# One graph-attention layer on one core: k made transposed by one product a block, and turned back

## The chip, the cores and the metric

The kernel runs on one core of one Trainium2 chip. The metric is the device time of one execution in microseconds (us). A core has five engines that run their own instruction streams in order and wait for each other by semaphores: TensorE (PE, matrix products and transposes, its weight loads listed apart as PEld), VectorE (DVE), ScalarE (ACT), GpSimd (POOL), and SyncE (SP), which issues DMAs here. PE works from SBUF and writes into PSUM; DVE and ACT read both.

## The reference

There are 12,500 nodes with 128 features, 212,500 edges sorted by `dst`, and 128 features for each edge. Eight heads of 16 features each:

```python
h = relu(layernorm(x))
q = h @ Wq.T + bq
k = edge_attr @ Wk.T + bk
v = h @ Wv.T + bv
in_m, out_m, diag_m = sum(q[src] * k), sum(q[dst] * k), sum(q[src] * q[dst])   # over each head
score = (softmax_by_dst(in_m / 4) + softmax_by_dst(out_m / 4) + softmax_by_dst(diag_m / 4)) * edge_weight ** lam
out = x + leaky_relu(segment_sum(score * v[dst], dst) @ Wo.T + bo, 0.1)
```

## The kernel before

After a first part over the nodes (their norm, `q`, and the two tables `q_table` and `q3_table` in DRAM), the main loop runs over 415 blocks of 512 edges. A block is four columns (`JN = 4`) of 128 edges, one edge a partition. Five blocks (`S = 5`, one of each fifth of the edge list) make one step `t`, and `g = 5 t + s` counts blocks. The features of five blocks come in one DMA into `ea` (`fetch_edges`, 1,280 KB).

For each block the loop needs three things in the layout "edge on the partition": `qs = q[src]`, `qd = q[dst]` and `k`.

- `gather` (line 652) fetches `q[src]`: four indirect DMAs a block on POOL (line 656), `LOOK = 12` blocks ahead. Each of the four also waits for a product of PE recorded in `behind`, so that the gathers run close behind PE's products: the gathers that are issued in iteration `g` wait for four places in PE's order of iteration `g - 1`.
- `spread_q` (line 1137) makes `q[dst]`: four bf16 products of one-hot rows (`oh`, made by ACT in `one_hots`, lines 1118 and 1119) with a window of the table, and ACT copies the result to SBUF (line 1144).
- `turn` (line 1121) transposes the edge features: four f32 transposes into the PSUM tile `eT_ps` (line 1124, one buffer), which ACT copies into `eT` (line 1126). `project` (line 1129) makes `k`: one bf16 product of ones with the bias (line 1131), then four f32 products with `eT` as the weights and `wk` as the moving operand (line 1133), all into `k_ps` (two buffers). A f32 product is two MATMULs in the trace, a transpose is one.

`logits` (line 1147) is DVE's: three products of 128x512 elements (lines 1152 to 1154, the first needs `qd` and `k_ps`, the last frees `k_ps`) and one reduction (line 1155).

The order of each engine is fixed by hand: `pin` ties every instruction behind the one that was recorded before it on the same engine. In iteration `g`, PE gets `spread_q(g + 1)`, `project(g + 1)`, `turn(g + 2)`, and then the work that comes once a step: transposes of the logits (`s = 0`), of the maxima (`s = 2`), `show_ends` (`s = 3`), `to_rows` with 16 f32 MATMULs (`s = 4`), and the nodes' products. ACT gets, in the same order, the copy of `qd_ps`, the copy of `eT_ps`, the two passes of `one_hots(g + 3)` and the work of the step. PE's order therefore asks of ACT once a block: the transposes of one block are copied by ACT before the product of that block, one iteration later, can run.

Of the kernel before, what the change touches and what calls it, by code (L numbers as in the profile page):

```python
# [472 lines left out]
def ordered_path(ctx: ExitStack, tc: tile.TileContext, flag, x, src, dst, edge_attr, edge_weight,  # L473
# [87 lines left out]
    wq, wv, wk, wo = [consts.tile([P, F], F32, name=n) for n in ("wq", "wv", "wk", "wo")]  # L561
    b3 = consts.tile([3, 3, F], BF, name="b3")
    bv3, bk3, bo3 = [b3[:, i, None, :].to_broadcast([3, JN, F]) for i in range(3)]
    bq_all = consts.tile([P, F], F32, name="bq_all")

    inv = consts.tile([P, NI], F32, name="inv")
# [23 lines left out]
    def pin(inst):  # L590

        engine = str(inst.ins.engine)
        if engine in pinned:
            tc.add_manual_dep(inst.ins, pinned[engine], mybir.DependencyInfo(
                mybir.DependencyClass.NoSync, mybir.DependencyReason.DATA), reason="in order")
        pinned[engine] = inst.ins.name
        return inst
# [47 lines left out]
    def fetch_edges(t):  # L645
        if t < G:
            ea = eas[t] = load.tile([P, S, JN * F], F32, name="ea")
            pin(nc.sync.dma_start(
                ea, edge_attr[:end * BE, :].rearrange("(s b p j) f -> p s b (j f)", s=S, b=G, p=P)
                [:, :, t, :]))  # L650
# [46 lines left out]
    with tc.tile_pool(name="prep", bufs=1) as prep, \  # L697
# [24 lines left out]
        rows_in(dst_r[:, 1:RC + 1], dst, nc.sync)  # L722
        pin(nc.gpsimd.dma_start(dst_r[1:, 0:1], dst[RC - 1:(RW - 1) * RC:RC, None]))
        pin(nc.gpsimd.dma_start(dst_r[:RW - 1, RC + 1:], dst[RC:(RW - 1) * RC + 1:RC, None]))
        b_row = prep.tile([1, 3, F], F32, name="b_row")
        for i, b in enumerate((bv, bk, bo)):
            pin(nc.sync.dma_start(b_row[:, i, :], b[None, :]))
# [286 lines left out]
    class Nodes:  # L1014
# [39 lines left out]
        def turn(self, to):  # L1054
            for b in range(self.n):
                pin(nc.tensor.transpose(to[:, b, :], self.h[:, b, :], ident))
            if self.hT is None:
                self.hT = fin.tile([P, JN, P], F32, name="hT")
            pin(nc.scalar.copy(self.hT[:, :self.n], to[:, :self.n]))
# [48 lines left out]
    with tc.tile_pool(name="work", bufs=2) as work, \  # L1108
            tc.tile_pool(name="scan", bufs=2) as scan, \
            tc.tile_pool(name="ps", bufs=1, space=PSUM) as ps:  # L1110
        ks, eTs, qds, q_ps, ohs, lTs = {}, {}, {}, {}, {}, {}

        def one_hots(g):

            if g < end:
                oh = ohs[g] = work.tile([K3, BE], BF, name="oh", bufs=5)
                d = st[g // S]["relb"][:, g % S, :]
                pin(nc.scalar.activation(d, d, AF.Abs, bias=before[:K3]))  # L1118
                pin(nc.scalar.activation(oh, d, AF.Relu, bias=1.0, scale=-1.0))  # L1119

        def turn(g):
            eT_ps = ps.tile([P, JN, P], F32, name="eT_ps", bufs=1)
            for j in range(JN):
                pin(nc.tensor.transpose(eT_ps[:, j, :], eas[g // S][:, g % S, j * F:(j + 1) * F], ident))  # L1124
            eT = work.tile([P, JN, P], F32, name="eT", bufs=3)
            pin(nc.scalar.copy(eT, eT_ps))  # L1126
            eTs[g] = eT

        def project(g):
            k_ps = ks[g] = ps.tile([P, JN, F], F32, name="k_ps", bufs=2)  # L1130
            pin(nc.tensor.matmul(k_ps, ones3, bk3, start=True, stop=False))  # L1131
            for j in range(JN):
                pin(nc.tensor.matmul(k_ps[:, j, :], eTs[g][:, j, :], wk, start=False,  # L1133
                                     stop=(j == JN - 1)))
            del eTs[g]

        def spread_q(g):
            s, d = g % S, st[g // S]
            qd_ps = q_ps[g] = ps.tile([P, JN, F], F32, name="qd_ps", bufs=2)
            for j in range(JN):  # L1140
                pin(nc.tensor.matmul(qd_ps[:, j, :], ohs[g][:, j * P:(j + 1) * P],  # L1141
                                     d["win"][:, s, :], start=(j == 0), stop=(j == JN - 1)))
            qds[g] = work.tile([P, JN, F], F32, name="qd")
            pin(nc.scalar.copy(qds[g], qd_ps))  # L1144
            del ohs[g]
# [226 lines left out]
                        pin(nc.gpsimd.memset(of.more, 0.0))  # L1372

        def hold(of, name):
            of.held = ps.tile([P, JN, F], F32, name=name, bufs=1 if name == "eT_ps" else 2)
            of.product(of.held, bv3, wv)

        products = str(mybir.EngineType.PE)
# [3 lines left out]
        fetch_rows(1)  # L1382
        one_hots(0)
        turn(0)
        spread_q(0)
        project(0)
        turn(1)
        one_hots(1)
        one_hots(2)
        for g in range(end):  # L1390
            s, t = g % S, g // S
            nodes_before(t, s)
            gather(g + LOOK)
            if s == 0:
                fetch_edges(t + 1)
            if g + 1 < end:
                spread_q(g + 1)
                behind[g + 1, 0] = pinned[products]
                project(g + 1)
                behind[g + 1, 1] = pinned[products]  # L1400
            if g + 2 < end:
                turn(g + 2)
                behind[g + 1, 2] = pinned[products]
            logits(g)
            one_hots(g + 3)
            if s == 0:
                if t > 0:
                    turn_logits(t - 1)
                    scan_on(t - 1)
                later(select, t - 2)  # L1410
                later(spread_far, t - 2)
            elif s == 1:
                later(scan_back, t - 2)
                if t == 1:
                    logits_few()
            elif s == 2:
                later(turn_max, t - 2)
                later(powers, t - 2)
            elif s == 3:
                later(show_ends, t - 2)  # L1420
                later(weigh_powers, t - 2)
                fetch(t + 2)
            else:
                later(to_rows, t - 2)
            ahead, k = (t + 2, s - 3) if s > 2 else (t + 1, s + 2)
            if ahead > 1:
                fetch_rows(ahead, [k])
                fetch_places(ahead, [k])
            later(put_rows, t - 2 if s == 4 else t - 3, [(s + 1) % S])
            if t == G - 1:  # L1430
                if 0 < s < 4:
                    select(G - 3 + s)
                elif s == 4:
                    for i in (G - 2, G - 1, G):
                        show_ends(i)
            behind[g + 1, 3] = pinned[products]
            nodes_between(t, s)
            begin_rest(g - (end - LOOK))
            if g < S:
                of = [u for u in range(NU) if g in parts_of(u)]  # L1440
                pin(nc.scalar.dma_start(
                    sums[g][of[0] * UN:(of[0] + len(of)) * UN].rearrange(
                        "(n p) i c -> p n (i c)", p=P),
                    blank[:, None, :].to_broadcast([P, 2 * len(of), 2 * 2 * H3])))
# [6 lines left out]
        last_pair.scores()  # L1451
        last_pair.turn(small([P, JN, P], "node_ps"))
        scan_on(G - 1)
        hold(rest[0], "eT_ps")
        last_pair.project_v(ps.tile([P, JN, F], F32, name="k_ps", bufs=2))
        scan_back(G - 2)
        turn_max(G - 2)
# [84 lines left out]
```

## Time and profile before

| | |
|---|---|
| time, median of 3 runs | 2700.01 us (2693.41 to 2700.97) |
| profiled execution: its own time | 2699.03 us |
| profiled execution: span | 2697.2 us |
| main loop's blocks | 415 |
| POOL, gathers (line 656) | 1660 indirect DMAs, 1580.9 us busy |
| DVE, four instructions of `logits` | 280.7 + 282.7 + 282.9 + 727.5 us busy |

The span is the time from the first to the last instruction of the profiled execution; what lies around it is 1.8 us. "Idle before" in a row names the time in which the engine stood still before the instructions of that group, and what ended it: "remote" is an update of a semaphore that the profile can't put down to an instruction that had just ended, and "issue" a start for which it sees no wait.

### The profile page before, as it was taken

The page shows a single profiled execution, that of the slowest core. Times are in us where ns is not written, and L with a number is a line of the kernel's source. Part 1 is how long each engine was busy: PE and PEld are TensorE (multiplying, and loading weights), DVE is VectorE, ACT ScalarE, POOL GpSimd, SP SyncE. Part 2 cuts the span into 40 slices and gives each one's busy share as a digit, 9 for nine tenths or more (in the row PEclk, how much of TensorE's full clock was granted, in tenths as well). Part 3 has the DMA queues.
Part 4 walks back from the last instruction along what each step waited for, and adds up shares of the span by engine and source line. Part 5 has one row for each costly group of instructions (what it writes and reads, how often), then busy time and mean ns, then how long its engine had stood idle before and what let it go on. Part 6 is the DMA issues. An engine that isn't in the chain of part 4 may idle for free.

```text
span 2697.2 us, 35162 instructions
## 1 busy us (share of the span) xinstructions
PE 1792.3 (66%) x10209; PEld 1446.1 (54%) x10209; DVE 2000.0 (74%) x2582; ACT 1382.5 (51%) x2526; POOL 1616.2 (60%) x1690
## 2 busy tenths in 40 slices
PE   6136666666566676766767667676766767666776
PEld 5125555555455565555555556554555556555564
DVE  7647776777677777776877778778777787777794
ACT  6534554454445554555455455455554555555572
POOL 4656666666666666666666666666666666666610
PEclk9667776777777767787777777777777786877776
DMA  7764445444544454445444444444444444444431
GB/s 214 228 196 125 116 114 140 115 116 122 139 117 124 127 135 121 128 120 145 119 124 124 137 130 123 124 138 126 121 120 142 127 125 123 139 126 125 118 105 52
DMA packets 319110, 351.23 MB, mean 130 GB/s; under 512 B 137530, under 2 KB 238661, under 8 KB 318600
## 3 DMA queue, kind: packets, MB, share of 16 engines
q1 hardware_dynamic: 250141, 233.59, 29.2%
q0 software_dynamic: 53344, 109.11, 16.8%
q10 hardware_dynamic: 15424, 6.19, 0.9%
q8 instruction: 83, 1.36, 0.2%
q14 instruction: 118, 0.97, 0.1%
HBM read 316.50 MB, written 32.17 MB: 129 GB/s over the span
## 4 chain that ended last, share of the span: by engine, by line
PE 43%; issue 16%; ACT 14%; another core or an unknown queue 12%; DVE 11%; DMA 3%; SPq 1%; ACTq 0%; POOL 0%; DVEq 0%; POOLq 0%
PE k_ps L1133 15%; PE w_ps L1286 7%; PE eT_ps L1124 6%; PE qd_ps L1141 5%; PE k_ps L1131 3%; ACT eT L1126 3%; DVE u L1208 2%; ACT qd L1144 2%; ACT relb L1118 2%; PE node_ps L1064 2%; DMA q_table<-q 2%; PE m_ps L1238 2%; ACT oh L1119 2%; DVE prod L1153 1%
## 5 line engine op out<-in xcount | busy, mean ns | idle before, releaser
L656 POOL DMA_INDIRECT qq<-q_table,src_i x1660 | 1580.9, 952 | 916.0 <-issue 371.6
L1133 PE MATMUL k_ps<-wk,eT 128*128 128x128 f32 x3320 | 668.4, 363 | 583.0 <-issue 358.4
L1133 PEld LDWEIGHTS k_ps<-wk,eT 128*128 128x128 f32 x3320 | 567.4, 258 | 740.1 <-issue 457.8
L1155 DVE TENSOR_REDUCE lT<-prod 128x96 f32<-128x1536 f32 x415 | 727.5, 1753 | 14.4
L1126 ACT COPY eT<-eT_ps 128x512 f32<-128x512 f32 x415 | 244.0, 588 | 838.7 <-remote 602.5
L1152 DVE TENSOR_TENSOR prod<-qd,k_ps 128x512 f32<-128x512 f32 x415 | 280.7, 676 | 148.6 <-remote 82.9
L1124 PE MATMUL eT_ps<-ident,ea 128*128 128x128 f32 x1660 | 346.6, 348 | 1.2 <-DVE found L962 1.0
L1141 PE MATMUL qd_ps<-win,oh 126*128 126x128 bf16 x1660 | 191.7, 247 | 208.6 <-DMA q_table<-q 70.6
L1144 ACT COPY qd<-qd_ps 128x512 f32<-128x512 f32 x415 | 240.1, 579 | 152.5 <-remote 42.5
L1118 ACT ACTIVATE relb<-relb,before 126x512 bf16<-126x512 bf16 x415 | 301.8, 727 | 0.0
L1141 PEld LDWEIGHTS <-oh 126*128 126x128 bf16 x1660 | 149.3, 113 | 261.6 <-issue 180.0
L1154 DVE TENSOR_TENSOR prod<-qq,k_ps 128x512 f32<-128x512 f32 x415 | 282.9, 682 | 0.0
L1153 DVE TENSOR_TENSOR prod<-qq,qd_ps 128x512 f32<-128x512 f32 x415 | 282.7, 681 | 0.0
L1208 DVE TENSOR_TENSOR_SCAN u<-far,u,l_ps 120x512 f32<-120x512 bf16 x82 | 105.0, 1280 | 238.4 <-PE k_ps L1133 58.8
L1124 PEld LDWEIGHTS eT_ps<-ident,ea 128*128 128x128 f32 x1660 | 279.1, 186 | 1.7 <-DVE found L962 1.3
L1119 ACT ACTIVATE oh<-relb 126x512 bf16<-126x512 bf16 x415 | 261.5, 630 | 33.8 <-issue 20.6
L1286 PE MATMUL w_ps<-back,sel 128*126 128x144 f32 (+1 forms) x1344 | 229.6, 334 | 26.1 <-ACT sel L1276 13.5
L1286 PEld LDWEIGHTS w_ps<-back,sel 128*126 128x126 f32 (+1 forms) x1344 | 213.9, 230 | 48.2 <-ACT sel L1276 30.7
L1131 PE MATMUL k_ps<-b,ones 3*128 3x512 bf16 x415 | 183.4, 442 | 17.2 <-issue 8.5
L1246 DVE TENSOR_TENSOR back<-lT,m_ps 128x480 f32<-128x480 f32 x83 | 54.1, 652 | 166.3 <-PE eT_ps L1124 73.1
L1226 DVE TENSOR_TENSOR_SCAN m<-far_ps,head,u 120x512 f32<-120x512 f32 x81 | 103.3, 1275 | 0.0
L1291 ACT COPY rows<-w_ps 126x288 f32<-126x288 f32 x84 | 33.0, 393 | 127.7 <-PE qd_ps L1141 62.9
(194 smaller groups left out, 1449.1 us busy)
## 6 DMA issues: line engine op xcount, KB each, us to landing
ea<-in_edge_attr_dram SPq DMA_DIRECT2D x83, 1280.0 KB
relb<-rel_d SPq DMA_DIRECT2D x415, 126.0 KB
qq<-q_table,src_i POOLq DMA_INDIRECT x1660
win<-q_table SPq DMA_DIRECT2D x415, 31.5 KB
far<-far_d SPq DMA_DIRECT2D x84, 120.2 KB
q_table<-q SPq DMA_DIRECT2D x24, 384.0 KB
sums<-rows SPq DMA_DIRECT2D x412, 7.9 KB
q_table<-xq SPq DMA_DIRECT2D x24, 256.0 KB
```

The costliest lines, as they stand in the source:

```text
L656: rows = pin(nc.gpsimd.indirect_dma_start(out=qq[:, j, :], out_offset=None, in_=q_table, in_offset=bass.IndirectOffsetOnAxis(ap=src_i[:, g ...
L1118: pin(nc.scalar.activation(d, d, AF.Abs, bias=before[:K3]))
L1119: pin(nc.scalar.activation(oh, d, AF.Relu, bias=1.0, scale=-1.0))
L1124: pin(nc.tensor.transpose(eT_ps[:, j, :], eas[g // S][:, g % S, j * F:(j + 1) * F], ident))
L1126: pin(nc.scalar.copy(eT, eT_ps))
L1133: pin(nc.tensor.matmul(k_ps[:, j, :], eTs[g][:, j, :], wk, start=False, stop=(j == JN - 1)))
L1141: pin(nc.tensor.matmul(qd_ps[:, j, :], ohs[g][:, j * P:(j + 1) * P], d["win"][:, s, :], start=(j == 0), stop=(j == JN - 1)))
L1144: pin(nc.scalar.copy(qds[g], qd_ps))
L1153: pin(nc.vector.tensor_mul(prod[:, :, 1, :], qqs[g], q_ps[g]))
L1154: pin(nc.vector.tensor_mul(prod[:, :, 0, :], qqs[g], ks[g]))
L1155: pin(nc.vector.tensor_reduce(lTs[t][:, :, s, :], prod.rearrange("p j i (h d) -> p j (i h) d", d=DIM), AX.X, ALU.add))
L1286: pin(nc.tensor.matmul(w_ps[:, i].rearrange("p s c -> p (s c)"), d["sel"][:n, j, lo:lo + 3, :].rearrange("p s w -> p (s w)"), d["back"][:n ...
```

## The change

`k` is now made with the features on the partitions. `project` takes `wk` as the weights and all 512 columns of `eT` as the moving operand, in one f32 product into the PSUM tile `kT_ps`. ACT adds the bias in its copy to `kT` (the bias is one number a partition now, `bk_col`, loaded once at the start). The new `turn_k` transposes `kT` back, four f32 transposes into `k_ps`. The product with ones that brought the bias is gone. `eT_ps` and `kT_ps` share one PSUM buffer (`tag="turned"`, one buffer); `eT` has two buffers in place of three.

The order in iteration `g` becomes `project(g + 2)`, `spread_q(g + 1)`, `turn_k(g + 1)`, `turn(g + 3)`, so `k` runs through one more stage and the features are turned three blocks ahead. The four places that gathers wait for are now the ends of `project`, of `turn_k`, of `turn`, and of the iteration. `fetch_edges` is called at the end of a step for the step after the next.

```diff
+    bk_col = consts.tile([P, 1], F32, name="bk_col")
...
+        pin(nc.sync.dma_start(bk_col, bk[:, None]))
...
         def turn(g):
-            eT_ps = ps.tile([P, JN, P], F32, name="eT_ps", bufs=1)
+            eT_ps = ps.tile([P, JN, P], F32, name="eT_ps", tag="turned", bufs=1)
             for j in range(JN):
                 pin(nc.tensor.transpose(eT_ps[:, j, :], eas[g // S][:, g % S, j * F:(j + 1) * F], ident))
-            eT = work.tile([P, JN, P], F32, name="eT", bufs=3)
+            eT = work.tile([P, JN, P], F32, name="eT")
             pin(nc.scalar.copy(eT, eT_ps))
             eTs[g] = eT
 
         def project(g):
+            kT_ps = ps.tile([P, JN, P], F32, name="kT_ps", tag="turned", bufs=1)
+            pin(nc.tensor.matmul(kT_ps.rearrange("f j p -> f (j p)"), wk,
+                                 eTs.pop(g).rearrange("f j p -> f (j p)"), start=True, stop=True))
+            kTs[g] = work.tile([P, JN, P], F32, name="kT")
+            pin(nc.scalar.activation(kTs[g], kT_ps, AF.Identity, bias=bk_col))
+
+        def turn_k(g):
             k_ps = ks[g] = ps.tile([P, JN, F], F32, name="k_ps", bufs=2)
-            pin(nc.tensor.matmul(k_ps, ones3, bk3, start=True, stop=False))
             for j in range(JN):
-                pin(nc.tensor.matmul(k_ps[:, j, :], eTs[g][:, j, :], wk, start=False,
-                                     stop=(j == JN - 1)))
-            del eTs[g]
+                pin(nc.tensor.transpose(k_ps[:, j, :], kTs[g][:, j, :], ident))
+            del kTs[g]
...
         turn(0)
-        spread_q(0)
         project(0)
         turn(1)
+        spread_q(0)
+        turn_k(0)
+        project(1)
+        turn(2)
...
             gather(g + LOOK)
-            if s == 0:
-                fetch_edges(t + 1)
+            if g == 0:
+                fetch_edges(1)
+            if s == S - 1:
+                fetch_edges(t + 2)
+            if g + 2 < end:
+                project(g + 2)
+                behind[g + 1, 0] = pinned[products]
             if g + 1 < end:
                 spread_q(g + 1)
-                behind[g + 1, 0] = pinned[products]
-                project(g + 1)
+                turn_k(g + 1)
                 behind[g + 1, 1] = pinned[products]
-            if g + 2 < end:
-                turn(g + 2)
+            if g + 3 < end:
+                turn(g + 3)
                 behind[g + 1, 2] = pinned[products]
```

More of the change, by code (lines that the diff above doesn't have):

```diff
@@ L1110, in ordered_path @@
             tc.tile_pool(name="ps", bufs=1, space=PSUM) as ps:
-        ks, eTs, qds, q_ps, ohs, lTs = {}, {}, {}, {}, {}, {}
+        ks, eTs, kTs, qds, q_ps, ohs, lTs = {}, {}, {}, {}, {}, {}, {}
         def one_hots(g):
@@ L1374, in hold @@
         def hold(of, name):
-            of.held = ps.tile([P, JN, F], F32, name=name, bufs=1 if name == "eT_ps" else 2)
+            of.held = ps.tile([P, JN, F], F32, name=name, tag=name, bufs=1 if name == "turned" else 2)
             of.product(of.held, bv3, wv)
@@ L1453, in ordered_path @@
         scan_on(G - 1)
-        hold(rest[0], "eT_ps")
+        hold(rest[0], "turned")
         last_pair.project_v(ps.tile([P, JN, F], F32, name="k_ps", bufs=2))
```

## The prediction

> **What bounds the kernel now.** I read the page's busy shares first, then its groups with their idle times, the list of waits, and last the timelines of PE, ACT and POOL in one stretch of the main loop.
>
> ```profile
> span 2697.2 us, 35162 instructions
> PE 1792.3 (66%) x10209; PEld 1446.1 (54%) x10209; DVE 2000.0 (74%) x2582; ACT 1382.5 (51%) x2526; POOL 1616.2 (60%) x1690
> ...
> L656 POOL DMA_INDIRECT qq<-q_table,src_i x1660 | 1580.9, 952 | 916.0 <-issue 371.6
> L1133 PE MATMUL k_ps<-wk,eT 128*128 128x128 f32 x3320 | 668.4, 363 | 583.0 <-issue 358.4
> ...
> L1126 ACT COPY eT<-eT_ps 128x512 f32<-128x512 f32 x415 | 244.0, 588 | 838.7 <-remote 602.5
> ...
> L1124 PE MATMUL eT_ps<-ident,ea 128*128 128x128 f32 x1660 | 346.6, 348 | 1.2 <-DVE found L962 1.0
> ```
>
> No engine is full, so something makes them wait for each other. Two idle times stand out: 583.0 us of PE before the products of k, and 838.7 us of ACT before the copy of the features that these products need. The list of waits says what ACT waits for, the tile `prod` how long a block takes, and the cores' view the clock:
>
> ```profile
> ACT eT L1126 <- remote: 602.5, 134, 6.9
> ...
> PE qd_ps L1141 <- DMA q_table<-q: 70.6, 1, 70.6
> ```
>
> ```profile
> L1152 DVE TENSOR_TENSOR prod<-qd,k_ps x415: 654/680/690, 160.9 to 2629.1; 128x512 f32<-128x512 f32 x139
> ```
>
> ```profile
> core 0: 2697.2 us, clock 0.750
> ```
>
> A block takes (2629.1 - 160.9) / 414 = 5.96 us. The copy waits only for PE's transposes, and 134 times this wait lasts 602.5 / 134 = 4.5 us. The timelines show why:
>
> ```profile
> 1520.77 0.59 PE L1141 MATMUL qd_ps<-win,oh 126*128 126x128 bf16 x4 [3.04 <-DVE prod L1153]
> 1521.37 0.58 PE L1131 MATMUL k_ps<-b,ones 3*128 3x512 bf16 x1
> 1521.88 2.07 PE L1133 MATMUL k_ps<-wk,eT 128*128 128x128 f32 x8
> 1523.74 1.06 PE L1124 MATMUL eT_ps<-ident,ea 128*128 128x128 f32 x4
> 1524.60 1.01 PE L1238 MATMUL m_ps<-ident,m 120*128 120x120 f32 x4
> ...
> 1541.45 0.39 PE L1141 MATMUL qd_ps<-win,oh 126*128 126x128 bf16 x4
> 1541.77 0.39 PE L1131 MATMUL k_ps<-b,ones 3*128 3x512 bf16 x1
> 1542.08 1.16 PE L1133 MATMUL k_ps<-wk,eT 128*128 128x128 f32 x8
> 1543.08 0.60 PE L1124 MATMUL eT_ps<-ident,ea 128*128 128x128 f32 x4
> 1543.51 0.60 PE L1175 MATMUL l_ps<-ident,lT 128*120 128x128 f32 x4
> ...
> 1545.63 0.60 PE L1124 MATMUL eT_ps<-ident,ea 128*128 128x128 f32 x4
> ...
> 1554.20 2.08 PE L1133 MATMUL k_ps<-wk,eT 128*128 128x128 f32 x8 [6.25 <-issue]
> 1556.07 1.06 PE L1124 MATMUL eT_ps<-ident,ea 128*128 128x128 f32 x4
> ...
> 1559.41 0.60 PE L1124 MATMUL eT_ps<-ident,ea 128*128 128x128 f32 x4
> ```
>
> ```profile
> 1524.84 0.59 ACT L1126 COPY eT<-eT_ps 128x512 f32<-128x512 f32 x1 [2.86 <-issue]
> ...
> 1543.98 0.60 ACT L1126 COPY eT<-eT_ps 128x512 f32<-128x512 f32 x1
> ...
> 1553.57 0.59 ACT L1126 COPY eT<-eT_ps 128x512 f32<-128x512 f32 x1 [6.70 <-remote]
> ...
> 1557.17 0.59 ACT L1126 COPY eT<-eT_ps 128x512 f32<-128x512 f32 x1 [1.26 <-PE eT_ps L1124]
> ...
> 1563.98 0.58 ACT L1126 COPY eT<-eT_ps 128x512 f32<-128x512 f32 x1 [3.21 <-remote]
> ```
>
> ```profile
> 1521.26 0.94 POOL L656 DMA_INDIRECT qq<-q_table,src_i  x1 [2.15 <-issue]
> ...
> 1543.44 0.94 POOL L656 DMA_INDIRECT qq<-q_table,src_i  x1 [1.67 <-PE k_ps L1133]
> ...
> 1550.93 0.94 POOL L656 DMA_INDIRECT qq<-q_table,src_i  x1 [0.30 <-issue]
> 1553.80 0.94 POOL L656 DMA_INDIRECT qq<-q_table,src_i  x1 [1.93 <-remote]
> ...
> 1561.29 0.94 POOL L656 DMA_INDIRECT qq<-q_table,src_i  x1 [0.30 <-issue]
> 1564.15 0.94 POOL L656 DMA_INDIRECT qq<-q_table,src_i  x1 [1.92 <-remote]
> ```
>
> PE's transposes end at 1545.63 + 0.60 = 1546.23, but ACT starts to copy at 1553.57. POOL's last gather of a run ended at 1550.93 + 0.94 = 1551.87, 1.70 us before. The next time: transposes end at 1560.01, POOL's last gather at 1562.23, the copy starts at 1563.98, 1.75 us later. So while POOL issues gathers in a row, the word that PE is done reaches the others late, and it comes through some 1.7 us after POOL has run out of gathers that it may issue (each waits for a place in PE's order). Not at once, though: the transposes that ended at 1524.80 (3.5 us into the run that began at 1521.26), at 1543.68 (0.2 us into the next) and at 1557.13 (3.3 us into the third) were copied 0.04 to 0.30 us later. Those that ended 2.8 us (1546.23) and 6.2 us (1560.01) into a run were not. I call a word from PE that passes "in time", the other "held". This link is read from the rows; what carries it I can't see.
>
> That gives the block's account. Six gathers on from 1543.44 POOL is at 1550.93: 1.248 us each, 4.99 us for a block's four. The other 5.96 - 4.99 = 0.97 us are pauses. A pause in the quoted rows costs (1.67 + 1.93 + 1.92) / 3 - 0.30 = 1.54 us, so 0.97 / 1.54 = 0.63 of the blocks pay one. The loop is set by POOL's runs and the pauses between them, and the pauses by how many hand-overs from PE get through inside one run.
>
> **The change part by part.** *PE's work.* From start to start in the rows, in the fast and the slow stretch: the bias product 0.31 and 0.51 us, the eight MATMULs of k 1.00 and 1.86, four transposes 0.43 and 0.86. The bias goes. The one product streams 512 f32 columns twice. No row has it; from below it is two bf16 passes of 512 columns (2 x 0.31 = 0.62; 2 x 0.51 = 1.02), from above the eight MATMULs as they are. Nearest is a transpose, one f32 pass of 128 columns: 8 x 0.43 / 4 = 0.86 and 8 x 0.86 / 4 = 1.72. I take these. Four transposes are added. Net: -0.31 - 0.14 + 0.43 = -0.02 fast, -0.51 - 0.14 + 0.86 = +0.21 slow; at a mean clock of 0.75 half and half, +0.10 us a block, 40 us over 414. Bounds: -0.26 and -0.49 at the lower price, +0.12 and +0.35 at the upper. PE is busy 66%, so this counts only inside a hand-over.
>
> *ACT's work.* One more pass over 128x512 a block, like line 1126: 588 ns, 415 x 0.588 = 244 us, 51% to 60%. It lies in ACT's idle time (838.7 us before the copy alone). Free of the cover it would cost 244 us. In ACT's order it stands ahead of the copies of `qd` and `eT`, so these now wait for PE's product too.
>
> *The hand-overs.* Before, a block has one in the loop: transposes, word to ACT, copy, product in the next iteration. After, there are two, one behind the other: transposes, word, copy to `eT`, product, word, biased copy to `kT`, and only then the next transposes, since both tiles share one PSUM buffer. From the release of a held word to the end of the next transposes it is now 0.59 (copy) + 1.00 or 1.86 + 0.43 or 0.86 = 2.0 to 3.3 us. After it is 0.59 + 0.86 or 1.72 + 0.32 or 0.60 (`spread_q`, start to start) + 0.43 or 0.86 (`turn_k`) + 0.43 or 0.86 = 2.6 to 4.6 us; the copy to `kT` hides behind `spread_q` and `turn_k` if its own word is in time. So the second word leaves PE some 1.0 us later in POOL's run. The rows have words in time up to 3.5 us and held ones from 2.8 us: a shift of 1.0 us moves it across. DVE gains nothing: `turn_k(g + 1)` stands behind `project(g + 2)` on PE, which waits for the copy.
>
> The price: 0.37 of the blocks pay no pause now. From below none of these is lost, 0 us; from above all, 0.37 x 1.54 = 0.57 us a block, x 414 = 236 us. The quoted cases at 2.8 to 3.5 us split (two pass, one is held), so I take half: 118 us.
>
> The Trainium skill, "Perfetto Trace Analysis", section Matmuls, says that independent groups of products should rotate through PSUM banks, so that emptying one overlaps the next group's products. Here the change does the opposite. By that rule alone every block would pay the copy, 414 x 0.588 = 243 us, near the upper bound; before, the buffer is single too, and the trace shows 1.2 us of waiting ahead of all transposes (line 1124), so a single buffer alone is no wait here.
>
> *What costs nothing.* The load of `bk_col` is one small DMA among the first ones on SP; the two further stages at the start fall into the 70.6 us in which PE waits for the table. `fetch_edges` moves by one iteration, but the transposes that need it move with it, and the buffer that it fills was read three iterations before in both orders. SP holds behind it the windows and rows of later steps, which are as early as before. If that cover fails, a late `ea` would stop PE, at most once in five blocks.
>
> *Sum.* 2699 (the execution: span 2697.2 and 1.8 around it, 1 us under the median) + 118 = 2817, and the median's 1 us: 2818 us.
>
> **The rivals.** *All second words are held* (the shared buffer makes every block pay a pause): 2700 + 236 = 2936. For it: two words a block must pass; against: the first leaves PE early in the run.
>
> *Words pass as now, and only work is added*: PE's 40 us show, 2740. For it: one word passed 3.5 us into a run. Against: the shift of 1.0 us.
>
> *Faster: the wide product is cheap.* If it streams at the bias product's pace, PE does 0.26 (fast) to 0.49 us (slow) less a block ahead of the second word, 0.375 on the mean; 414 x 0.375 = 155 us if all of it is on the path, 78 us at half: 2622. It decides from a product under 0.31 + 1.00 - 0.43 = 0.88 us (fast) and 0.51 + 1.86 - 0.86 = 1.51 us (slow); place: the stretch from the copy to the next transposes. For it: weights are loaded once a block in place of four times, and fewer words from PE could be held. Against: in the rows four f32 transposes take 0.43 us where four bf16 products of the same width (`spread_q`) take 0.32, so f32 columns pass more slowly.
>
> The Trainium skill, "TensorE: Matmul & The Clock Gate", section Back-to-back issue gap, gives 131 ns for 512 columns against 81 ns for 128 in a stream. By it two passes would take an estimated 0.26 us and this rival would hold more than fully. The trace disagrees for f32: here a pass of 128 columns takes 108 to 215 ns (a quarter of the transposes).
>
> *No change*: POOL's own pace and pauses hide all of it, 2700.
>
> **How the numbers follow.** Half of the blocks lose: 0.44, 2818, its own range 2740 to 2900. All lose: 0.12. Work alone: 0.14. Faster: 0.25. No change: 0.05. Within 0.3% (8 us) is no change for a measurement of this kernel. So slower 0.70, same 0.05, faster 0.25. The range of 2630 to 2950 leaves out half of the faster case (0.13) and the far end of the worst (0.06).
>
> **What would show it.** On the page: line 1131 gone, a product of 512 f32 columns with two MATMULs a block, of 0.86 to 1.72 us a pair, PE's share about as before, ACT's near 60%. In the waits: those of the two copies for PE together over 602.5 us, in more than 134 cases. In POOL's timeline: more pauses, runs of four to five gathers rather than of six to seven. I am wrong if the waits that end as "remote" get fewer, if POOL's idle time falls under 916.0 us, or if the extra time appears in DVE's waits for gathered rows.

## The result, and the profile after

| | before | after |
|---|---|---|
| time, median | 2696.71 us (2691.79 to 2700.97, 4 runs) | 2735.79 us (2732.57 to 2739.15, 4 runs) |
| ratio to before on the same chip, 95% interval | | 1.0146 (1.012 to 1.0171) |
| span of the profiled execution | 2697.2 us | 2732.4 us |

Slower by 39 us between the medians, 35 us between the profiled spans. The forecast was 118 us more than before. The page of after, its busy shares and the groups that answer to those of before (busy us, mean ns | idle time before, and what ended most of it):

```profile
span 2732.4 us, 32733 instructions
...
PE 1752.5 (64%) x8964; PEld 1194.8 (44%) x8964; DVE 2005.8 (73%) x2582; ACT 1654.6 (61%) x2941; POOL 1616.0 (59%) x1690
...
L657 POOL DMA_INDIRECT qq<-q_table,src_i x1660 | 1580.8, 952 | 945.6 <-issue 356.3
L1133 PE MATMUL kT_ps<-eT,wk 128*128 128x512 f32 x830 | 594.1, 805 | 514.0 <-ACT eT L1128 298.0
...
L1126 PE MATMUL eT_ps<-ident,ea 128*128 128x128 f32 x1660 | 325.1, 328 | 391.5 <-ACT kT L1136 249.8
L1128 ACT COPY eT<-eT_ps 128x512 f32<-128x512 f32 x415 | 243.2, 586 | 405.8 <-remote 199.0
...
L1136 ACT ACTIVATE kT<-kT_ps,bk_col 128x512 f32<-128x512 f32 x415 | 282.6, 681 | 152.0 <-PE kT_ps L1133 50.9
```

The bias product is gone, the wide product stands there with two MATMULs a block (830), ACT is at 61%. POOL's idle time before its gathers rose by 945.6 - 916.0 = 29.6 us, most of the 35 us (as it must when the loop gets longer and the gathers are as busy as before). The copy of the features waits far less for a late word than before (199.0 us, once 602.5). PE now waits in two places, 514.0 us before the product and 391.5 us before the transposes, where it waited 583.0 and 1.2 us. The tile `prod` gives the block, the cores' view the clock:

```profile
L1159 DVE TENSOR_TENSOR prod<-qd,k_ps x415: 658/680/690, 157.4 to 2663.9; 128x512 f32<-128x512 f32 x139
```

```profile
core 0: 2732.4 us, clock 0.808
```

(2663.9 - 157.4) / 414 = 6.05 us a block, 0.09 more than before, 38 us over the loop. The list of waits of after (us in total, times, longest):

```profile
PE kT_ps L1133 <- ACT eT L1128: 298.0, 114, 6.7
...
PE eT_ps L1126 <- ACT kT L1136: 249.8, 151, 12.3
POOL qq L657 <- remote: 203.4, 120, 2.6
ACT eT L1128 <- remote: 199.0, 58, 6.6
...
ACT kT L1136 <- remote: 42.1, 23, 13.2
```

The two copies together wait 199.0 + 42.1 = 241 us in 81 cases for late words, where the forecast had over 602.5 us in over 134. A third copy of ACT, that of `qd`, went the other way. Its rows, before and after:

```profile
ACT qd L1144 <- remote: 42.5, 15, 5.1
```

```profile
ACT qd L1151 <- remote: 103.1, 31, 5.8
```

The timelines of after show a held word and one that passes:

```profile
1530.79 0.39 PE L1148 MATMUL qd_ps<-win,oh 126*128 126x128 bf16 x4
1531.02 0.61 PE L1141 MATMUL k_ps<-ident,kT 128*128 128x128 f32 x4
1532.21 0.66 PE L1126 MATMUL eT_ps<-ident,ea 128*128 128x128 f32 x4 [0.58 <-issue]
1537.28 2.08 PE L1133 MATMUL kT_ps<-eT,wk 128*128 128x512 f32 x2 [4.42 <-issue]
1539.15 0.63 PE L1148 MATMUL qd_ps<-win,oh 126*128 126x128 bf16 x4
1539.57 1.06 PE L1141 MATMUL k_ps<-ident,kT 128*128 128x128 f32 x4
1540.43 1.06 PE L1126 MATMUL eT_ps<-ident,ea 128*128 128x128 f32 x4
...
1542.16 1.16 PE L1133 MATMUL kT_ps<-eT,wk 128*128 128x512 f32 x2
1543.16 0.39 PE L1148 MATMUL qd_ps<-win,oh 126*128 126x128 bf16 x4
1543.39 0.60 PE L1141 MATMUL k_ps<-ident,kT 128*128 128x128 f32 x4
1546.25 0.66 PE L1126 MATMUL eT_ps<-ident,ea 128*128 128x128 f32 x4 [2.26 <-ACT kT L1136]
```

```profile
1536.64 0.58 ACT L1128 COPY eT<-eT_ps 128x512 f32<-128x512 f32 x1 [4.01 <-remote]
...
1541.53 0.58 ACT L1128 COPY eT<-eT_ps 128x512 f32<-128x512 f32 x1 [0.97 <-issue]
...
1544.01 0.60 ACT L1254 ACTIVATE back<-back 128x480 f32<-128x480 f32 x1 [0.62 <-DVE back L1253]
1545.51 0.69 ACT L1136 ACTIVATE kT<-kT_ps,bk_col 128x512 f32<-128x512 f32 x1 [0.89 <-PE k_ps L1141]
```

```profile
1533.93 0.94 POOL L657 DMA_INDIRECT qq<-q_table,src_i  x1 [0.30 <-issue]
1536.82 0.94 POOL L657 DMA_INDIRECT qq<-q_table,src_i  x1 [1.95 <-remote]
```

The transposes that end at 1532.21 + 0.66 = 1532.87 are copied at 1536.64, 1.77 us after POOL's last gather of the run ended (1534.87): held, as before. Those that end at 1541.49, 4.67 us into the run that began at 1536.82, are copied 0.04 us later. The next copy shows PE's new wait: the biased copy starts at 1545.51, 2.19 us after its product ended (1542.16 + 1.16), and PE stands 2.26 us before the transposes that need the same buffer. Two things make this up. ACT's work of the step, `back`, stands ahead of the copy until 1544.61, and then ACT waits 0.89 us more, though the product ended at 1543.32: by the measure below a held word. The product's pair, start to start, takes 1.00 us (1542.16 to 1543.16) and 1.87 us (1537.28 to 1539.15).

From the traces I also counted, in the main loop, POOL's pauses (over 0.45 us between two gathers) and the words of PE that left it inside a run of gathers. "Held" is a copy that starts more than 0.6 us after both PE's end and the end of ACT's work before it. In the last columns are only words for which ACT's work before had ended by then, or at most 0.5 us later.

```
kernel             gathers  pauses  gathers a run  mean pause | word   held of all   held, ACT idle
before             1484     268     5.5            1.65 us    | eT     174 of 331    96 of 190
after              1489     287     5.2            1.64 us    | eT      95 of 358    88 of 292
                                                              | kT      36 of 342     2 of 135
```

The new word, that of the product for `kT`, is held in about one case of ten (of the words that found ACT free 2 of 135, or 13 of 211 if ACT's work may end 0.6 us later). The word for `eT` is held about half as often as before. The word of `spread_q` for the copy of `qd`, counted in the same way, is held 55 times of 339 before and 84 of 339 after.

### The profile page after: what moved, and what is told of

Read it like the earlier page. It is cut to its first block, busy times and chain, and to the rows that moved or that the text cites. A ratio compares the mean times of both kernels' runs of the same rounds, so it can differ in the third digit from the quotient of the medians.

```text
span 2732.4 us, 32733 instructions
## 1 busy us (share of the span) xinstructions
PE 1752.5 (64%) x8964; PEld 1194.8 (44%) x8964; DVE 2005.8 (73%) x2582; ACT 1654.6 (61%) x2941; POOL 1616.0 (59%) x1690
## 4 chain that ended last, share of the span: by engine, by line
PE 48%; ACT 22%; issue 14%; another core or an unknown queue 10%; DVE 4%; DMA 1%; SPq 1%; ACTq 0%; DVEq 0%
PE kT_ps L1133 15%; PE eT_ps L1126 9%; PE w_ps L1293 7%; PE k_ps L1141 6%; ACT kT L1136 5%; ACT eT L1128 4%; PE qd_ps L1148 3%; ACT qd L1151 3%; ACT relb L1120 3%; ACT oh L1121 3%; PE d_ps L1279 2%; ACT sel L1282 2%; PE m_ps L1245 2%; PE node_ps L1066 1%
## 5 line engine op out<-in xcount | busy, mean ns | idle before, releaser
L657 POOL DMA_INDIRECT qq<-q_table,src_i x1660 | 1580.8, 952 | 945.6 <-issue 356.3
L1133 PE MATMUL kT_ps<-eT,wk 128*128 128x512 f32 x830 | 594.1, 805 | 514.0 <-ACT eT L1128 298.0
L1126 PE MATMUL eT_ps<-ident,ea 128*128 128x128 f32 x1660 | 325.1, 328 | 391.5 <-ACT kT L1136 249.8
L1128 ACT COPY eT<-eT_ps 128x512 f32<-128x512 f32 x415 | 243.2, 586 | 405.8 <-remote 199.0
L1126 PEld LDWEIGHTS eT_ps<-ident,ea 128*128 128x128 f32 x1660 | 225.6, 167 | 477.0 <-ACT kT L1136 299.3
L1133 PEld LDWEIGHTS kT_ps<-eT,wk 128*128 128x128 f32 x830 | 156.0, 234 | 600.6 <-ACT eT L1128 336.2
L1136 ACT ACTIVATE kT<-kT_ps,bk_col 128x512 f32<-128x512 f32 x415 | 282.6, 681 | 152.0 <-PE kT_ps L1133 50.9
L1141 PE MATMUL k_ps<-ident,kT 128*128 128x128 f32 x1660 | 314.2, 323 | 1.0 <-issue 0.7
L1148 PEld LDWEIGHTS <-oh 126*128 126x128 bf16 x1660 | 157.6, 116 | 330.6 <-issue 319.5
L1141 PEld LDWEIGHTS k_ps<-ident,kT 128*128 128x128 f32 x1660 | 222.9, 171 | 1.6 <-issue 1.2
L1293 PEld LDWEIGHTS w_ps<-back,sel 128*126 128x126 f32 (+1 forms) x1344 | 220.7, 236 | 1.7 <-issue 1.1
```

The costliest lines, as they stand in the source:

```text
L657: rows = pin(nc.gpsimd.indirect_dma_start(out=qq[:, j, :], out_offset=None, in_=q_table, in_offset=bass.IndirectOffsetOnAxis(ap=src_i[:, g ...
L1133: pin(nc.tensor.matmul(kT_ps.rearrange("f j p -> f (j p)"), wk, eTs.pop(g).rearrange("f j p -> f (j p)"), start=True, stop=True))
L1136: pin(nc.scalar.activation(kTs[g], kT_ps, AF.Identity, bias=bk_col))
L1141: pin(nc.tensor.transpose(k_ps[:, j, :], kTs[g][:, j, :], ident))
L1293: pin(nc.tensor.matmul(w_ps[:, i].rearrange("p s c -> p (s c)"), d["sel"][:n, j, lo:lo + 3, :].rearrange("p s w -> p (s w)"), d["back"][:n ...
```

## The experiments

The runs fell on chips of two kinds, told apart by the time of the kernel before beside them. Beside a "before" of 2669 to 2697 us words are held, as in the profile shown. Beside a "before" of 2250 to 2254 us the traces taken (of variants of the two kernels, not of the kernel before itself) show none held, and with all its gathers POOL goes on at 1.25 us a gather, with one pause in all of them together. Whether this belongs to the chip isn't shown: chip number 1 stands beside 2250.62 us in some runs and beside 2695.77 us in later ones. So each experiment is read against the kernel before on its own chip, which its paragraph names.

**One hand-over taken off the path.** The kernel before, with the features turned three blocks ahead and nothing else of the change:

```diff
-            eT = work.tile([P, JN, P], F32, name="eT", bufs=3)
+            eT = work.tile([P, JN, P], F32, name="eT", bufs=4)
...
+        turn(2)
...
-            if s == 0:
-                fetch_edges(t + 1)
+            if g == 0:
+                fetch_edges(1)
+            if s == S - 1:
+                fetch_edges(t + 2)
...
-            if g + 2 < end:
-                turn(g + 2)
+            if g + 3 < end:
+                turn(g + 3)
```

> The kernel before, with one part of the change alone: the features are turned three blocks ahead (four eT buffers, the edge load called one iteration earlier), k is made as before. Held words (a word from PE waits for the end of POOL's run, and a block pays for it only where its hand-over is on the path): the word of the transposes has one iteration more, so the copy is off the path; remote waits of the copy of eT may stay, but PE's idle time before the products of k (583 us) falls under 200 us and the time to 2450 to 2600 us. Rival, added work alone explains the change: no work is added or removed here, 2690 to 2705 us.

> The kernel before with the features turned three blocks ahead and k made as before, once more. Held words: beside a kernel before of 2697 us the copy has one iteration more, so PE idles less than 200 us before the products of k and the time is 2450 to 2600 us; beside one of 2250 us no change, as in the first look. Rival: no change in either, ratio 0.998 to 1.002.

Beside 2250.01 us: 2249.61 us, ratio 0.9999 (0.9988 to 1.0009). Beside 2669.34 us: 2683.61 us, 1.0057 (1.004 to 1.0073). A hand-over less on the path gives nothing on either chip. The waits of the second run:

```profile
ACT eT L1126 <- remote: 538.7, 123, 19.5
...
PE eT_ps L1124 <- issue: 261.8, 100, 17.3
POOL qq L656 <- remote: 246.3, 144, 2.5
...
DVE prod L1152 <- remote: 202.6, 91, 9.4
```

The words for `eT` are held as often as before, though the product has a block's time to spare. Then others wait instead: DVE 202.6 us, and PE stands before its transposes. I counted 267 pauses of 1.61 us in 1482 gathers, as before the change. So what sets the pauses isn't the one word that the prediction followed, and the forecast of 2450 to 2600 us failed.

**The bias alone.** The kernel before without the bias product (`k` lacks its bias):

```diff
-            pin(nc.tensor.matmul(k_ps, ones3, bk3, start=True, stop=False))
```

> The kernel before without the product of ones that adds the bias to k (the bias of k is left out of the output). Tells the price of the part that the change removes from PE. Held words: 0.31 to 0.51 us less ahead of the next transposes in every block, so fewer of them are held: 2600 to 2680 us, and the remote waits of the copy of eT fall under 500 us. Rival, PE's work doesn't matter, POOL and the waits do: 2685 to 2705 us.

Beside 2250.01 us: 2250.91 us, 1.0004 (0.9995 to 1.0014). On this chip POOL's gathers hide it, so it tells nothing of the other.

**Gathers without a limit.** POOL no longer waits for places in PE's order, in the kernel before and in the changed one:

```diff
-                if (g - LOOK, j) in behind:
+                if False:
```

> The kernel before, with gathers that no longer wait for places in PE's order (only for their buffers). Held words: POOL's runs get longer, so words of PE are held for longer, and the time rises over 2800 us. Rival, the waits of the gathers cost pauses and hold nothing: POOL's idle time falls and the time is under 2650 us.

> The changed kernel with gathers that no longer wait for places in PE's order. Held words: two hand-overs a block, so it loses more than the kernel before does in the same experiment: over 2850 us. Rival, pauses of POOL are what a block pays for: under 2690 us.

> The kernel before with gathers that no longer wait for places in PE's order, once more: the first look fell beside a kernel before of 2250 us, where POOL never paused and no word of PE was held. Beside one of about 2690 us: held words by long runs of POOL say over 2800 us; if it is POOL's waiting for PE itself that goes with held words, POOL runs at 1.25 us a gather without pauses and the time is 2250 to 2300 us. Beside 2250 us: 2245 to 2255 us again.

> The changed kernel with free gathers, once more. Beside a kernel before of about 2690 us: over 2850 us if long runs hold words; 2255 to 2330 us if the waits of the gathers go with held words, a little over before_free_2 for the work that the change adds. Beside 2250 us: 2250 to 2262 us again.

> The kernel before with gathers that don't wait for places in PE's order, hoped to stand beside a kernel before of about 2690 us. There: over 2800 us if long runs of POOL hold PE's words; 2250 to 2300 us without pauses if POOL's waits for PE go with held words. Beside 2250 us: the same 2245 to 2255 us.

| | time, us | before beside it | ratio |
|---|---|---|---|
| before, free | 2250.19 | 2250.01 | 0.9998 (0.9988 to 1.0008) |
| after, free | 2256.48 | 2250.01 | 1.0027 (1.0016 to 1.0038) |
| before, free, again | 2249.69 | 2250.62 | 0.9999 (0.999 to 1.0009) |
| after, free, again | 2260.91 | 2250.62 | 1.0046 (1.003 to 1.0061) |
| before, free, other chip | 3019.14 | 2670.24 | 1.1299 (1.1279 to 1.132) |

The last row is the test of the link that the prediction read from the rows. POOL may issue as many gathers in a row as its buffers allow, and the same kernel takes 13% longer. Its waits:

```profile
POOL qq L656 <- DVE prod L1154: 703.4, 145, 11.1
ACT eT L1126 <- remote: 697.7, 103, 12.7
```

ACT waits up to 12.7 us for a word, and POOL itself stops for buffers that DVE has not freed. The words don't all wait for such a stop: of 121 words for `eT` held here, 35 were copied while POOL's run still went on, and 18 between 1.4 and 2.1 us after its last gather. Runs grew from 5.5 to 9.8 gathers, pauses from 1.65 to 4.59 us (152 in 1491 gathers). On the 2250 us chip, with the same waits removed, none of 401 words of the transposes was held (counted in "after, free", first run), and POOL never paused. So PE's words are held with POOL's runs on one kind of chip, and not on the other. Whether it is POOL's issuing or the gathers' own transfers that does it isn't separated.

**Half the gathers.** Two of the four gathers of a block are replaced by one plain DMA of fixed rows, in the kernel before and in the changed one:

```diff
+            pin(nc.sync.dma_start(
+                qq[:, 2:, :].rearrange("p (u k) f -> p u (k f)", k=2), units(q_table, 0, 1, F)))
-            for j in range(JN):
+            for j in range(2):
```

> The kernel before with two of the four gathers of a block left out; fixed rows come by a plain DMA instead (the output is of these rows). It takes POOL's floor of 4.99 us a block away (2.5 us are left). If POOL's pace sets the block: beside 2250 us the time falls towards DVE's 1870 / 414 = 4.52 us a block, 2070 to 2150 us; beside 2697 us held words get shorter too, 2250 to 2450 us. Rival, POOL doesn't set it: within 1% of the kernel before.

> The changed kernel with the same two gathers left out. With POOL's floor gone the two hand-overs a block and the added work show, if they cost anything: 1 to 5% over half_before. Rival, they lie in idle time whatever POOL does: within 0.5% of half_before.

Beside 2669.34 us: 2110.24 us, 0.7902 (0.7888 to 0.7915), and 2256.89 us, 0.8468 (0.8442 to 0.8494). Beside the same 2669.34 us the changed kernel itself ran again:

> The changed kernel, unchanged. The four runs before had the kernel before at 2250 us where the blind profile was of 2697 us, and no wait of the copy of eT ended as remote. If held words are what the change costs, a run beside a kernel before of 2250 us shows no cost: 2245 to 2260 us, ratio 0.998 to 1.005; beside one of 2697 us it repeats 2736 us, ratio 1.012 to 1.017. Rival, the added work of PE and ACT costs the 37 us wherever it runs: ratio 1.014 to 1.018 beside 2250 us too.

2722.51 us, 1.021 (1.0188 to 1.0231): 53 us over before. It is slower again, and its waits for late words are again few. With half the gathers the words pass. The kernel before came out faster than the 2250 to 2450 us expected, and the two kernels 7% apart, where 1 to 5% were expected. The waits of the kernel before with half its gathers, then of the changed one (lines have moved by two):

```profile
ACT eT L1128 <- PE eT_ps L1126: 263.4, 161, 3.1
...
ACT eT L1128 <- remote: 1.7, 1, 1.7
```

```profile
PE eT_ps L1128 <- ACT kT L1138: 262.1, 130, 10.7
...
ACT eT L1130 <- remote: 2.2, 1, 2.2
```

The copy of the features meets one late word in the whole run, of 1.7 and of 2.2 us. Without POOL's floor the change costs 2256.89 - 2110.24 = 147 us, nearly three times the 53 us that it costs with all gathers. The wait that it brings is PE's before the transposes, for the copy that empties the shared buffer, 262.1 us; with all gathers it was 249.8 us, and 182.7 us in the repeat. So the change's longer chain is real, and with all gathers most of its cost is covered. The tile `prod` gives the blocks, before and after:

```profile
L1154 DVE TENSOR_TENSOR prod<-qd,k_ps x415: 659/679/689, 140.8 to 2039.3; 128x512 f32<-128x512 f32 x139
```

```profile
L1161 DVE TENSOR_TENSOR prod<-qd,k_ps x415: 658/680/690, 144.7 to 2180.6; 128x512 f32<-128x512 f32 x139
```

The kernel before takes (2039.3 - 140.8) / 414 = 4.59 us a block, and DVE is busy for 1847.89 us of this stretch, 97%: there DVE sets the pace. The changed kernel takes 4.92 us a block. That lies just under the 4.99 us of a block's four gathers.

**The shared bank.** `kT_ps` gets a PSUM buffer of its own. It takes the place of one of the three buffers of the small tiles; the controls take only that third buffer away. All four are the changed kernel, two with half its gathers:

```diff
-            kT_ps = ps.tile([P, JN, P], F32, name="kT_ps", tag="turned", bufs=1)
+            kT_ps = ps.tile([P, JN, P], F32, name="kT_ps", tag="kT_ps", bufs=1)
...
-            return ps.tile(shape, F32, name=name, tag="small", bufs=3)
+            return ps.tile(shape, F32, name=name, tag="small", bufs=2)
```

> half_after (two of four gathers left out) with a PSUM bank of its own for kT_ps, taken from the small tiles (two buffers in place of three). If the shared bank makes the 147 us by which half_after stood over half_before (PE waited 262 us for the biased copy ahead of the next transposes), this one is at 2110 to 2170 us and that wait is under 50 us. Rival, the longer chain through ACT or the work itself makes it: within 1% of half_after_two.

> half_after with the small tiles' two buffers alone, the shared bank kept: tells what the lost small buffer costs. If little, 2250 to 2275 us as half_after; if the small buffer is what counts, over 2300 us, and then half_after_own is read against this one.

> The changed kernel with a PSUM bank of its own for kT_ps (small tiles with two buffers in place of three). Beside a kernel before of about 2690 us: if the shared bank makes the cost of the change, the time is 2660 to 2710 us, ratio 0.995 to 1.005, less what the lost small buffer costs; if held words do, 2720 to 2760 us as before. Beside 2250 us POOL's 4.99 us a block covers all: 2245 to 2265 us.

> The changed kernel with two PSUM buffers in place of three for the small tiles, all else as it is; it is the control of after_own (1.0278 of before beside 2670.24 us). If the shared bank costs something at four gathers a block, this one lies clearly above after_own: by 131 us times the share of blocks without a pause at most, so up to 1.06 of before beside some 2670 to 2700 us. If POOL's runs and the held words set the block, the bank gives nothing back there: 1.02 to 1.03, as after_own. Beside 2250 us, where no word is held: 1.003 to 1.006 as after_free_2 and e4_after_free, since POOL alone sets the block.

| | time, us | before beside it | ratio |
|---|---|---|---|
| half the gathers, own bank | 2186.0 | 2250.62 | 0.9721 (0.9705 to 0.9737) |
| half the gathers, shared bank | 2316.91 | 2250.62 | 1.0321 (1.0267 to 1.0375) |
| all gathers, own bank | 2748.29 | 2670.24 | 1.0278 (1.0251 to 1.0304) |
| all gathers, shared bank | 2320.64 | 2253.82 | 1.0308 (1.0263 to 1.0354) |

With half the gathers the bank alone is worth 131 us, on the chip where no word is held. The kernel with its own bank still stands 76 us over the kernel before with half its gathers (2110.24 us, on another chip; 2110 to 2170 us were expected), so the bank isn't the whole cost. The lost small buffer costs time by itself: 2316.91 us, where the changed kernel with half its gathers and three of them took 2256.89 us on another chip. The last two rows fell on chips of different kinds, so at all gathers the bank by itself stays open on the chip where words are held. What the last row does show: on the 2250 us chip, the changed kernel with two small buffers takes the same with all gathers as with half of them. There its own chain sets the time, not POOL, against the forecast of 1.003 to 1.006:

```profile
PE eT_ps L1126 <- ACT kT L1136: 316.5, 228, 5.3
```

And where words are held, an own bank, with one small buffer less, didn't bring the changed kernel back to 2670 us; the words for `eT` were held more again:

```profile
ACT eT L1128 <- remote: 407.1, 128, 6.4
```

**The limit moved.** The gathers wait for a place one block later or one block earlier in PE's order (in the tighter ones, the call of `gather` also moves to the end of the iteration):

```diff
-                if (g - LOOK, j) in behind:
-                    tc.add_manual_dep(rows.ins, behind[g - LOOK, j], mybir.DependencyInfo(
+                if (g - LOOK + 1, j) in behind:
+                    tc.add_manual_dep(rows.ins, behind[g - LOOK + 1, j], mybir.DependencyInfo(
```

> The kernel before with each gather waiting for a place one block later in PE's order. If the places set the length of POOL's runs and these hold the words: beside a kernel before of about 2670 us runs fall to one to four gathers, words pass, waits of the copy of eT that end as remote fall under 200 us, and the time is 2250 to 2500 us. Rival, hand-overs set the pauses: as many held words, and POOL later: 2690 to 2900 us. Beside 2250 us (no words held): 2250 to 2400 us, POOL's own waits showing.

> The changed kernel with each gather waiting for a place one block later. If words then pass, the change's own chain through ACT and the shared bank shows as it does at half the gathers, beside either kind of kernel before: 4 to 9% over tight_before. Rival, the chain lies hidden behind POOL: within 2% of tight_before.

> The kernel before with each gather waiting for a place one block earlier in PE's order. If the places set the runs: longer runs, longer held words; beside about 2670 us the time lies between that and the 3019 us without any places, 2720 to 2950 us. Rival, hand-overs set the pauses: 2650 to 2690 us. Beside 2250 us: 2245 to 2255 us.

| | time, us | ratio to 2695.77 us beside it |
|---|---|---|
| before, tighter | 2693.33 | 0.9985 (0.9975 to 0.9996) |
| after, tighter | 2731.59 | 1.0135 (1.0115 to 1.0156) |
| before, looser (`g - LOOK - 1`) | 2695.96 | 1.0003 (0.999 to 1.0016) |

A block's shift either way does nothing: 263 and 261 pauses, against 268. The forecasts by which the places set the runs (2250 to 2500 us tighter, 2720 to 2950 us looser) both failed. The changed kernel stays 1.4% over the kernel before when both are tighter, so its chain doesn't come out here as it does with half the gathers. The waits of the tighter and of the looser kernel differ little from the 602.5 us and 134 times before:

```profile
ACT eT L1126 <- remote: 590.2, 128, 8.7
```

```profile
ACT eT L1126 <- remote: 604.5, 138, 7.0
```

That there is a limit is worth 13% here; where it stands within a block is worth nothing. It may be that POOL only runs so much later along with PE; no run tests this. No version with all its work done beat the kernel before by more than this 0.15%.

## Why the prediction was right in its sign and wrong in its size

*Right: what bounds the kernel before.* POOL's runs of gathers and the pauses between them, with PE's words held during the runs. Free gathers (3019 us) and half the gathers (2110 us) move the time the way this says. Half the gathers also take away POOL's floor, so their gain isn't that of the words alone. That the word for `eT` is what sets the pauses was not borne out (turned ahead: no gain).

*Near: the prices of the single parts.* The product was priced 0.86 and 1.72 us and took 1.00 and 1.87 us in the rows above, which is the upper bound of the prediction and not its price. The transposes back took 0.86 us in the slower stretch (1539.57 to 1540.43), as priced. ACT went to 61%. Its biased copy takes 681 ns where the plain one takes 586, 0.09 us more than I took, 39 us of ACT over the run. The rival of a cheap wide product fell with that price.

*Wrong: the term of 118 us.* The step that failed is "a shift of 1.0 us moves it across", with "half" of the 0.37 blocks without a pause lost to the second word. The sign held, the size didn't. The counts say 268 pauses in 371 blocks before (0.72, where I had 0.63 from three pauses) and 287 in 372 after (0.77): of the 0.28 blocks without a pause 0.05 were lost, a fifth and not a half. At 1.64 - 0.30 = 1.34 us each that is 0.05 x 1.34 x 414 = 28 us, and POOL's idle time rose by 29.6. The fifth is of this trace only. In the repeat of the changed kernel there are 317 pauses in 371 blocks (0.85), nearly the half, but they last 1.48 us. Beyond 0.30 us each, all pauses of 371 blocks add up to 363 us before and to 385 and 374 us in the two traces after. So there are more pauses, but in the repeat they are shorter, and a fixed price for each lost block doesn't hold.

*Wrong: what was put at nothing.* That "the copy to `kT` hides behind `spread_q` and `turn_k` if its own word is in time" failed as well, and with it ACT's new pass as one that lies in idle time: the word is in time in about nine cases of ten, and still PE waits 249.8 us in 151 cases for this copy before the next transposes. The prediction took from the 1.2 us before them that a single buffer is no wait; with two tiles that take turns in it, it is one.

*Why it was so few.* I took a word's place in time in POOL's run to decide whether it passes, from five cases of which the two latest to pass left at 3.3 and 3.5 us. The "second word" of the prediction is that of the next transposes, for `eT`. It does leave later: of the words that found ACT free, 63 of 188 left PE more than 4 us into a run before, and 172 of 293 after. So the shift came. But of these late ones 55 of 63 were held before, and only 76 of 172 after; the one at 4.67 us above passed. From 2 to 4 us into a run, 40 of 97 words for `eT` were held before, and none of 84 words for `kT` after. So a place in time alone doesn't decide, though early words hardly wait (1 of 28 held under 2 us before). What does decide stays open. It isn't enough that PE has work behind the word that can run at once, as it has behind the product's word (`spread_q`, `turn_k`). In the kernel with the features turned ahead `spread_q` and `project` stand like this behind the transposes' word, and it was held 164 times of 369. One case, PE and then ACT:

```profile
1520.31 0.79 PE L1124 MATMUL eT_ps<-ident,ea 128*128 128x128 f32 x4
...
1522.13 1.16 PE L1133 MATMUL k_ps<-wk,eT 128*128 128x128 f32 x8
```

```profile
1526.86 0.59 ACT L1126 COPY eT<-eT_ps 128x512 f32<-128x512 f32 x1 [5.95 <-remote]
```

The transposes ended at 1521.10, PE went on with the next products until 1523.29, and the copy came at 1526.86.

*The signs.* I had named fewer remote waits as a sign against me, and they got fewer: 241 us for both copies. With the copy of `qd` it is 344 us, against 645 us before. More pauses and shorter runs came as forecast. So the sign was right while the held words, by which it was forecast, got fewer; in that the prediction was lucky. That the time still rose has its reading in PE's two waits: held words gave way to waits for ACT's copies through the shared buffer (249.8 us with all gathers, 262.1 us with half, 337.3 us when gathers are free on the other chip, where no word is held at all). ACT's order puts the work of a step ahead of the copy to `kT`, as `back` in the rows above, and some of these waits are held words themselves. How much of the 35 us is this and how much is held words isn't separated.

```profile
PE eT_ps L1126 <- ACT kT L1136: 337.3, 231, 5.2
```

(This is the changed kernel with free gathers, its first run.)

*The rivals.* "Words pass as now, and only work is added" gave 2740 us, the nearest number, but by another way: it let PE's 40 us show, and PE's busy time fell by that much, 1792.3 to 1752.5, at a higher granted clock. "All second words are held" was the reverse of what the counts show. "No change" is near the truth on a chip of the other kind, where the change costs 0.3 to 0.5% with free gathers; the changed kernel as it stands was not run there.

*The rule on banks.* The trace of half the gathers bears it out where gathers don't set the pace: 131 us for a bank of its own. The 243 us by that rule (the Trainium skill, "Perfetto Trace Analysis", section Matmuls) counted the copy in every block, about twice that. With all gathers, where words are held, the whole change costs 39 and 53 us in its two measurements, whatever part of this the bank is.

## What to carry to other kernels

A floor that another engine sets takes most of the cost of a longer chain: before pricing an added hand-over, ask what time the chain would give by itself, and measure it by thinning out the floor (here half the gathers: +147 us, where +53 showed on the same chip). A threshold read from five cases of a timeline is no price: count all cases in the trace, for each word by itself, before a term hangs on it. And where one engine's long runs hold up another's signals, a limit on the runs is worth more than its exact place: 13% against 0.15% here.

## What the runs showed of the hardware

The same kernel takes 2250 to 2254 us beside some of the experiments and 2669 to 2697 us beside others; I call these two kinds of chip. On the first none of the words counted was late by more than 0.6 us, however long POOL issued gathers in a row. On the second 174 of 331 words for `eT` were late in the kernel before, more than half: 94 of them were copied 1.4 to 2.1 us after the last gather of the run, as in the rows of the prediction, but 42 while the run still went on. When nothing limits the runs, ACT waits up to 12.7 us for one. POOL's idle time before its gathers is 513 us on the one and 916.0 us on the other, which is most of the difference:

```profile
L656 POOL DMA_INDIRECT qq<-q_table,src_i x1660 | 1586.1, 955 | 512.7 <-issue 438.8
```

(The kernel before with free gathers, on a chip of the first kind.) What carries the words, and in what the chips or their states differ, stays open: no run here could look at it.
